# A deformable-convolution layer on one Trainium2 core: scratch copies tripled, one stage of work moved forward by part of an image

## The chip, the cores and the metric

The kernel runs on one core of one Trainium2 chip. The metric is the device time of one execution in microseconds (us); lower is better. All data are float32.

## The reference, cut to what matters

The program is a chain of four residual layers over a batch of 8 images of 384 channels and 32 x 32 pixels. Each layer adds to x the result of a block on the group-normalized x: attention over pixels (layer 0), three deformable depthwise convolutions with a channel gate (layer 1), attention over channels (layer 2), a sum of large depthwise convolutions (layer 3). Only layer 1 matters here:

```python
def deform_block(x, ow, ob, dw, pw, pb, K):
    pad = K // 2
    offsets = conv2d(x, ow, ob, pad)            # 2*K*K offset channels per pixel
    out = deform_depthwise(x, offsets, dw, K, pad)
    return conv2d(out, pw, pb, 0)               # 1x1

def deform_depthwise(x, offsets, w, K, pad):
    # for every tap k: sample x bilinearly at (pixel + tap + offset_k), zero outside,
    # multiply by the channel's weight w[:, k], and add up over the K*K taps
    ...

c3, c5, c7 = jnp.split(x, 3, axis=1)            # 128 channels each
out3 = deform_block(c3, ..., 3)
out5 = deform_block(c5, ..., 5)
out7 = deform_block(c7, ..., 7)
out = jnp.concatenate([out3, out5, out7], axis=1)
return out * se_weight(out, fc1_w, fc2_w)
...
x = x + layer1(group_norm(x))
```

## The kernel before, in words

Layers 0, 2 and 3 stand before and after layer 1 in the program and are not changed. Layer 1 (`layer1`) does bilinear sampling as matrix products. It walks 8 images (`b`), in each the three kernel sizes 3, 5 and 7 (`r` = 0, 1, 2; "kernel of 7" is r = 2), and in each kernel size the output columns in strips (`s`): four strips for 3, four for 5, ten for 7. The taps' rows are taken in groups: one group for 3, two for 5 and two for 7. A task is one (image, kernel size, strip, group); an image has 4 + 8 + 20 = 32 of them.

What a task needs is prepared by two stages that run beside the tasks, each ahead of them:

- `offsets(b, r)`: normalizes the 128 channels, transposes them on TensorE (line 569), writes them as small overlapping patches into a DRAM scratch image (`im`, line 593), and makes the offsets with one matmul per tap (line 621: 9 taps for 3, 25 for 5, 49 taps in two halves for 7). The weights of these matmuls (`cw`, line 549) are loaded `AHEAD` chunks in front. The positions (`pos`) go to DRAM (line 639).
- `hats(b, r)`: turns positions into bilinear weights, called hats. For each kx, and for 7 for each of two parts (rows and columns), one piece: load `d` from `pos` (line 657), take the absolute distance on ScalarE (line 673), take max(0, 1 - distance) on ScalarE (line 685), write the result to the DRAM scratch `hat` (line 703). The loads of `d` run one piece in front.

The tasks then do the sampling:

- `load_columns` (line 745, SyncE's queue) and `load_rows` (line 765, GpSimd's queue) bring the hats of task i + 2 from DRAM (`hx` and `s`), `patches` (line 721, GpSimd's queue) brings the patches `xw`.
- `sample_weights` spreads the column hats over partitions with a selection matrix on TensorE (`columns`, line 786; the matrix is `sel`, whose entries `SEL` lists) and multiplies them into the row hats on VectorE (line 789).
- `sample` multiplies patches with these weights on TensorE (`v`, line 826); ScalarE copies the sums out (`z`, line 834).
- `accumulate` multiplies by the tap's weight and adds on VectorE (`acc`, line 860).
- `end` does the 1 x 1 convolution (line 880, taken out by line 881) and, after the kernel of 7, the channel gate; it reads the results and x again (`or`, `xr`) and writes x back (line 922).

The order of all instructions in layer 1 is written out by hand (`manual_schedule`), so that each engine and each DMA queue runs them in program order. For each slot of a task the loop works out how much of the image is `done`, once by a measure called `room` and once by one called `cost`, and then advances each stage until it has as many steps as `PLAN` asks for. `PLAN` holds points (done, share of the stage's work), one list for offsets (by room) and one for hats (by cost), and is read by straight lines between points. In cost the kernel of 3 ends at 0.1 of an image, that of 5 at 0.381.

By these points the hats of the kernel of 7 of the next image are made from 0.79 of an image to 0.31 of the next one, and the hats of 3 and 5 from 0.31 to 0.79. The offsets run 1.3 images in front of the tasks, so that those of the kernel of 7 of the next image begin as the image begins.

The scratch images and hats have two copies, chosen by `b % 2`. Those of images are zeroed at their borders in layer 0 by `clear`, on GpSimd's queue.

Of the kernel before, what the change touches and what calls it, by code (L numbers as in the profile page):

```python
# [40 lines left out]
class Cells:  # L41
# [69 lines left out]
SEL = [(w, m, j) for w in sorted({c.wx for c in CELLS}) for m in range(1, 32 // w + 1) for j in range(m)]  # L111
SGAP = 32
WCH = 4
AHEAD = 5
# [29 lines left out]
def kernel(ctx: ExitStack, tc: tile.TileContext, t, out):  # L144
# [341 lines left out]
    def layer1(x2):  # L486
        with tc.tile_pool(name="l1w", bufs=1) as wp, tc.tile_pool(name="l1", bufs=2) as sp, tc.tile_pool(
# [24 lines left out]
            for i in range(2):  # L512
                h = wp.tile([P, max(g.pitch for g in CELLS) * H], F32, tag=f"hs{i}", name=f"hs{i}")
                nc.vector.memset(h, 0.0)
                hs.append(h)
# [3 lines left out]
            for i in range(3):  # L519
                s = wp.tile([P, SROW + 2 * SGAP], F32, tag=f"s{i}", name=f"s{i}")  # L520
                nc.vector.memset(s, 0.0)
                weights.append(s)
# [12 lines left out]
            def offsets(b, r):  # L535
# [25 lines left out]
                im = images[r, b % 2]  # L561
# [75 lines left out]
                pos = dpool.tile([n2, N], F32, tag=f"pos{r}", name=f"pos_{b}_{r}", bufs=2)  # L637
# [4 lines left out]
            def hats(b, r):  # L642
# [9 lines left out]
                def load(kx, part):  # L652
                    d = sp.tile([P, N], F32, tag="d", name=f"d_{b}_{r}_{kx}_{part[0]}")
                    at = 0
                    for a in part:
                        w = (g.wy, g.wx)[a]
                        nc.sync.dma_start(
                            d[at : at + ks * w],
                            bass.AP(
                                tensor=pos.tensor, offset=pos.offset + (2 * kx + a) * N, ap=[[0, w], [2 * ks * N, ks], [1, N]]  # L660
                            ),
                        )
                        at += ks * w
                    return d, at

                ahead = load(*todo[0])
                yield
                for j, (kx, part) in enumerate(todo):
                    d, n = ahead
                    if j + 1 < len(todo):  # L670
                        ahead = load(*todo[j + 1])
# [23 lines left out]
                    for a in part:  # L695
                        w = (g.wy, g.wx)[a]
                        for hat, lo in zip(hatsof[r, a, b % 2], (0, g.last and g.last[0])):
                            if not lo <= kx < lo + hat.shape[3]:
                                continue
                            s0 = 0 if hat is hatsof[r, a, b % 2][0] else g.strips - 1  # L700
# [9 lines left out]
            def patches(b, r, s):  # L710
# [5 lines left out]
                im = images[r, b % 2]  # L716
# [14 lines left out]
            def load_columns(i, b, r, s, k0, k1):  # L731
# [5 lines left out]
                tiles = hatsof[r, 1, b % 2]  # L737
# [15 lines left out]
            def load_rows(i, b, r, s, k0, k1):  # L753
# [5 lines left out]
                tiles = hatsof[r, 0, b % 2]  # L759
# [807 lines left out]
```

## Time and profile before

| | us |
|---|---|
| median of three runs | 8086.81 |
| lowest and highest | 8068.79, 8088.71 |
| the profiled execution's own time | 8090.77 |
| its span, first to last instruction | 8088.9 |

| engine in the span | busy us | share |
|---|---|---|
| PE (matmul) | 6941.8 | 86% |
| DVE (VectorE) | 3995.6 | 49% |
| ACT (ScalarE) | 2448.4 | 30% |
| POOL (GpSimd) | 1087.7 | 13% |

The mean granted TensorE clock is 0.896 of full speed. The DMA queues moved 1119 MB; the queue of GpSimd took 26.0% of the 16 engines' span and that of SyncE 19.9%. Layer 1 runs from about 2440 to 6690 us, some 510 us an image once it is under way.

A row of busy time by stretches gives, for each engine, the busy us and the number of instructions. A line in the chain of waits gives start, length and what the chain went through. In a timeline the brackets at the end of a line hold the engine's idle time before it and what ended that. SP and SPq are SyncE and its DMA queue; PEld is the load of a matmul's weights.

### The profile page before, as it was taken

How to read it: one execution, taken by the hardware profiler on the slowest of the kernel's cores; microseconds unless marked ns; L12 is line 12 of the kernel's file. 1: busy time of each engine (PE TensorE's matmuls, PEld its weight loads, DVE VectorE, ACT ScalarE, POOL GpSimd, SP SyncE). 2: the span in 40 equal slices, each digit the busy share in tenths (PEclk: the TensorE clock that was granted, in tenths of full speed). 3: DMA queues.
4: the chain of work that ended last, by engine and by line, in shares of the span. 5: the costliest groups of instructions: out<-in, count | busy, mean ns of one | idle time of the engine just before them, and what ended most of it. 6: DMA issues, size and time to landing. Idle time of an engine off the chain costs nothing.

```text
span 8088.9 us, 99749 instructions
## 1 busy us (share of the span) xinstructions
PE 6941.8 (86%) x38761; PEld 3835.8 (47%) x38761; DVE 3995.6 (49%) x7839; ACT 2448.4 (30%) x4587; POOL 1087.7 (13%) x2052
## 2 busy tenths in 40 slices
PE   8999999999986798798998989989799786888664
PEld 4434444444433355455555545555456464545342
DVE  4433433334332356575766757667577682222322
ACT  2232332332222333433434334343344330111000
POOL 0000000000001022222222222222222220000001
PEclk9999999999987898898988989989898887888787
DMA  1110000000006677878878788787887851000343
GB/s 55 23 48 29 20 10 22 20 7 15 15 22 197 185 208 203 256 220 257 233 206 273 218 258 235 216 274 216 259 237 224 242 155 69 32 32 16 96 117 115
DMA packets 529699, 1119.27 MB, mean 138 GB/s; under 512 B 160208, under 2 KB 386872, under 8 KB 489828
## 3 DMA queue, kind: packets, MB, share of 16 engines
q0 software_dynamic: 150880, 626.06, 26.0%
q1 hardware_dynamic: 370688, 467.37, 19.9%
q10 hardware_dynamic: 7652, 19.38, 0.7%
q8 instruction: 310, 5.08, 0.3%
q14 instruction: 169, 1.38, 0.1%
HBM read 888.01 MB, written 223.77 MB: 137 GB/s over the span
## 4 chain that ended last, share of the span: by engine, by line
PE 69%; DMA 15%; DVE 8%; issue 3%; ACT 2%; SPq 1%; POOL 1%; ACTq 0%; DVEq 0%; POOLq 0%
PE v L826 14%; PE po L621 10%; PE columns L786 7%; PE s L400 6%; PE s L384 6%; PE pa L409 6%; PE pqk L1255 3%; DMA s<-hat 3%; PE pc L1369 2%; DMA hx<-hat 2%; PE pq L368 2%; DVE acc L860 2%; PE po L439 2%; PE pk L368 2%; DMA xw<-im 2%
## 5 line engine op out<-in xcount | busy, mean ns | idle before, releaser
L826 PEld LDWEIGHTS v<-s,xw 120*128 120x128 f32 (+1 forms) x10560 | 1624.0, 204 | 1130.5 <-issue 645.5
L826 PE MATMUL v<-s,xw 120*128 120x126 f32 (+6 forms) x10560 | 1949.7, 327 | 210.8 <-ACT z L834 96.9
L834 ACT ACTIVATE z<-v 128x336 f32<-128x336 f32 (+6 forms) x2360 | 1095.0, 473 | 2383.6 <-PE v L826 2199.6
L860 DVE SCALAR_TENSOR_TENSOR acc<-z,dw,acc 128x128 f32<-128x128 f32 (+6 forms) x4504 | 1677.4, 377 | 125.4 <-ACT z L834 0.5
L789 DVE TENSOR_TENSOR s<-s,columns 120x896 f32<-120x896 f32 (+3 forms) x816 | 936.2, 1147 | 1387.6 <-PE columns L786 1266.1
L386 DVE TENSOR_REDUCE mx<-s 128x1 f32<-128x512 f32 x1024 | 640.4, 683 | 1109.3 <-PE s L384 1108.8
L621 PE MATMUL po<-xp,cw 128*98 128x512 f32 (+2 forms) x2944 | 1088.8, 592 | 16.1 <-ACT off L629 8.9
L786 PE MATMUL columns<-hx,sel 30*120 30x448 f32 (+6 forms) x3776 | 862.9, 599 | 238.5 <-DMA hx<-hat 134.1
L765 POOL DMA_DIRECT2D s<-hat x960 | 509.4, 545 | 2947.2 <-PE v L826 1291.2
L402 ACT ACTIVATE e<-s 128x512 f32<-128x512 f32 x1024 | 537.3, 601 | 1046.9 <-PE s L400 1035.6
L721 POOL DMA_DIRECT2D xw<-im x864 | 466.4, 578 | 1848.4 <-DVE off L635 1787.4
L400 PE MATMUL s<-q,k 49*128 49x512 f32 x2048 | 600.0, 637 | 53.4 <-DMA q<-both 53.4
L384 PE MATMUL s<-k,q 49*128 49x512 f32 x2048 | 599.1, 668 | 5.3 <-ACT e L402 2.1
L409 PE MATMUL pa<-e,va 128*49 128x512 f32 x2048 | 549.3, 611 | 18.2 <-ACT e L402 18.2
L786 PEld LDWEIGHTS columns<-hx,sel 30*120 30x120 f32 (+3 forms) x3776 | 265.4, 193 | 616.7 <-issue 246.9
L384 PEld LDWEIGHTS s<-k,q 49*128 49x128 f32 x2048 | 331.7, 317 | 278.9 <-issue 171.0
L400 PEld LDWEIGHTS s<-q,k 49*128 49x128 f32 x2048 | 253.6, 199 | 317.4 <-issue 202.9
L1369 PE MATMUL pc<-xT,hk 32*32 32x232 f32 (+6 forms) x9984 | 239.9, 428 | 178.7 <-issue 99.6
L621 PEld LDWEIGHTS po<-xp,cw 128*98 128x98 f32 (+2 forms) x2944 | 300.6, 151 | 171.8 <-issue 126.3
L409 PEld LDWEIGHTS pa<-e,va 128*49 128x49 f32 x2048 | 117.4, 124 | 370.1 <-issue 326.3
L1369 PEld LDWEIGHTS pc<-xT,hk 32*32 32x32 f32 x9984 | 169.4, 112 | 248.9 <-issue 160.3
L1255 PE MATMUL pqk<-wqk,xn 128*128 128x384 f32 x768 | 271.9, 519 | 9.5 <-DVE xn L256 8.4
(145 smaller groups left out, 3985.3 us busy)
## 6 DMA issues: line engine op xcount, KB each, us to landing
s<-hat POOLq DMA_DIRECT2D x288, 448.0 KB, 9.6
xw<-im POOLq DMA_DIRECT2D x608, 208.0 KB, 10.0
s<-hat POOLq DMA_DIRECT2D x288, 336.0 KB, 7.0
s<-hat POOLq DMA_DIRECT2D x128, 540.0 KB, 9.5
s<-hat POOLq DMA_DIRECT2D x128, 360.0 KB, 8.5
hat<-hs SPq DMA_DIRECT2D x112, 378.0 KB
s<-hat POOLq DMA_DIRECT2D x128, 324.0 KB, 7.4
x<-x SPq DMA_DIRECT2D x24, 1536.0 KB
```

The costliest lines, as they stand in the source:

```text
L384: mm(ps[j], lhsT=q[rows, n:N:QCH], rhs=k[rows, hs], start=True, stop=True)
L386: nc.vector.tensor_reduce(mx[:, j, n, h : h + 1], ps[j], AX.X, ALU.max)
L400: mm(ps[j], lhsT=k[rows, n * P : (n + 1) * P], rhs=q[rows, hs], start=True, stop=True)
L402: nc.scalar.activation(state["e", n % 2, j][:, hs], ps[j], AF.Exp, scale=HD**-0.5)
L409: mm(pa[rows, halves[h]], lhsT=va[:, n, 2 * g + j, :], rhs=state["e", n % 2, j][:, halves[h]], start=(n == 0), stop=(n == QCH - 1),)
L621: mm(po[i * g.pm : (i + 1) * g.pm, :n], lhsT=cw[:, k, :], rhs=xp[:, y0 : y0 + n // W, x : x + W], start=(ky == 0 and kx == 0), stop=(ky == ...
L786: mm(columns[: g.q, c, :n], lhsT=sel[rows, k, : g.q], rhs=hx[rows, :n], start=True, stop=True)
L789: nc.vector.tensor_tensor(dst, dst, columns[: g.q, : g.parts, :n], ALU.mult)
L826: mm(dst[:, (lo - k0) * nk : (hi + 1 - k0) * nk, :, xl * g.tw : (xl + 1) * g.tw], lhsT=state["xw", b, r, s][: g.q, xl, p0 + j, :], rhs=rhs ...
L834: nc.scalar.activation(z[:, :, yy : yy + n * g.th, :].rearrange("p k (j t) x -> p j k (t x)", j=n), v.rearrange("p j (k f) -> p j k f", k= ...
L860: nc.vector.scalar_tensor_tensor(dst, z[:, (ky - k0) * nk + kx - first, ky - i0 * g.th : ky - i0 * g.th + H, bx : bx + x1_ + 1 - x0], dw[: ...
L1369: mm(ps[32 * j : 32 * j + 32, i, lo * B : hi * B], lhsT=hk[32 * i : 32 * i + 32, j, (RL - d) * PITCH : (RL - d) * PITCH + W], rhs=xT[32 * ...
```

## The change

It gives images, hats and positions three copies in place of two (`AT = 3`). It moves the points of `PLAN`: offsets run 1.55 images in front in place of 1.3; the hats of 3 and 5 of the next image are made from 0.31 to 0.62 of an image, those of 7 from 0.62 to 1.05. The weights by which `room` spreads offsets over the kernels of 3 and 5 go from 1.5 and 2 to 2 and 3. The loads of `d` run two pieces in front, with three buffers. `SEL` lists only the entries in use (seven in place of nine), the offset weights run 4 chunks in front in place of 5, and the memsets of `hs` and of the three weight buffers `s` are issued on GpSimd in place of VectorE.

```diff
-SEL = [(w, m, j) for w in sorted({c.wx for c in CELLS}) for m in range(1, 32 // w + 1) for j in range(m)]
+SEL = sorted(
+    {
+        (c.wx, m, j)
+        for c in CELLS
+        for k0, k1 in c.groups
+        for m in {min(c.deep, k1 + 1 - k) for k in range(k0, k1 + 1, c.deep)}
+        for j in range(m)
+    }
+)
 SGAP = 32
 WCH = 4
-AHEAD = 5
+AHEAD = 4
+AT = 3
 
 STEP = 0.3
 PLAN = (
-    ((0, 0.095), (0.035, 0.3), (0.22, 1.02), (0.78, 2.02), (1.3, 2.6), (B - 1.3, B)),
-    ((0, 0.15), (0.035, 0.15), (0.07, 0.388), (0.225, 0.388))
-    + tuple((b + x, b + y) for b in range(B) for x, y in ((0.31, 1.0), (0.79, 1.388)) if b + y <= B),
+    ((0, 0.095), (0.035, 0.3), (0.22, 1.02), (0.78, 2.02), (1.45, 3.0), (B - 1.55, B)),
+    ((0, 0.15), (0.035, 0.15), (0.07, 0.388), (0.225, 0.388), (0.31, 1.0), (0.79, 1.388), (1.28, 2.0))
+    + tuple((b + x, b + y) for b in range(1, B) for x, y in ((0.31, 1.0), (0.62, 1.388), (1.05, 2.0)) if b + y <= B),
 )
...
-        for i in range(2):
+        for i in range(AT):
             images[r, i] = dpool.tile([g.cols, g.wy, g.ny, P], F32, tag=f"im{r}{i}", name=f"im{r}{i}")
...
                 h = wp.tile([P, max(g.pitch for g in CELLS) * H], F32, tag=f"hs{i}", name=f"hs{i}")
-                nc.vector.memset(h, 0.0)
+                nc.gpsimd.memset(h, 0.0)
...
                 s = wp.tile([P, SROW + 2 * SGAP], F32, tag=f"s{i}", name=f"s{i}")
-                nc.vector.memset(s, 0.0)
+                nc.gpsimd.memset(s, 0.0)
...
-                im = images[r, b % 2]
+                im = images[r, b % AT]
...
-                pos = dpool.tile([n2, N], F32, tag=f"pos{r}", name=f"pos_{b}_{r}", bufs=2)
+                pos = dpool.tile([n2, N], F32, tag=f"pos{r}", name=f"pos_{b}_{r}", bufs=AT)
...
-                    d = sp.tile([P, N], F32, tag="d", name=f"d_{b}_{r}_{kx}_{part[0]}")
+                    d = sp.tile([P, N], F32, tag="d", name=f"d_{b}_{r}_{kx}_{part[0]}", bufs=3)
...
-                ahead = load(*todo[0])
+                ahead = [load(*todo[j]) for j in range(2)]
                 yield
                 for j, (kx, part) in enumerate(todo):
-                    d, n = ahead
-                    if j + 1 < len(todo):
-                        ahead = load(*todo[j + 1])
+                    d, n = ahead.pop(0)
+                    if j + 2 < len(todo):
+                        ahead.append(load(*todo[j + 2]))
...
-                steps = (1.5, 2, 7 if k0 else 4)[r] * (min((s + 1) * g.nc, g.nx) - s * g.nc) / g.nc
+                steps = (2, 3, 7 if k0 else 4)[r] * (min((s + 1) * g.nc, g.nx) - s * g.nc) / g.nc
```

The other places where `b % 2` chose a copy of hats or images read `b % AT` in the same way.

More of the change, by code (lines that the diff above doesn't have):

```diff
@@ L696, in hats @@
                         w = (g.wy, g.wx)[a]
-                        for hat, lo in zip(hatsof[r, a, b % 2], (0, g.last and g.last[0])):
+                        for hat, lo in zip(hatsof[r, a, b % AT], (0, g.last and g.last[0])):
                             if not lo <= kx < lo + hat.shape[3]:
                                 continue
-                            s0 = 0 if hat is hatsof[r, a, b % 2][0] else g.strips - 1
+                            s0 = 0 if hat is hatsof[r, a, b % AT][0] else g.strips - 1
                             ns = hat.shape[0]
@@ L715, in patches @@
                 state["xw", b, r, s] = xw
-                im = images[r, b % 2]
+                im = images[r, b % AT]
                 for x in range(s * g.nc, min((s + 1) * g.nc, g.nx)):
@@ L736, in load_columns @@
                 n = tap // g.parts
-                tiles = hatsof[r, 1, b % 2]
+                tiles = hatsof[r, 1, b % AT]
                 hat = tiles[0][s] if nk == g.ks else tiles[1][0]
@@ L758, in load_rows @@
                 wt = weights[i % 3]
-                tiles = hatsof[r, 0, b % 2]
+                tiles = hatsof[r, 0, b % AT]
                 hat = tiles[0][s] if nk == g.ks else tiles[1][0]
```

## The prediction

> **What bounds the kernel now.** I read the slices of the span first: layer 1 is the part from 2440 to 6690 us, with the DMA at 6 to 8 tenths and the PE at 8 to 9. Layers 0, 2 and 3 keep their code, so what follows is layer 1 alone. The ends of the three kernel sizes of an image are seen in the ACT rows of line 881 (4259, 4333, 4450 and 4767 us for image 3), so I asked for the busy time in exactly those stretches, and in the same stretches of the last image.
>
> ```profile
> 4261.00:4335.00 74.00, 49.24 (x240) 32.11 (x239) 34.46 (x54) 27.59 (x56) 16.07 (x31) 0.82 0.99 316
> 4335.00:4451.00 116.00, 107.81 (x461) 65.14 (x462) 84.08 (x129) 54.91 (x122) 28.29 (x54) 0.93 0.82 242
> 4451.00:4769.00 318.00, 297.12 (x1536) 175.31 (x1536) 214.57 (x507) 117.06 (x218) 80.60 (x153) 0.95 0.76 219
> 6251.00:6322.00 71.00, 39.90 (x218) 26.94 (x216) 34.30 (x53) 24.77 (x51) 16.16 (x31) 0.78 0.91 286
> 6322.00:6428.00 106.00, 92.17 (x427) 59.59 (x425) 84.45 (x130) 50.68 (x116) 26.49 (x50) 0.92 0.77 239
> 6428.00:6683.00 255.00, 211.39 (x1101) 152.31 (x1100) 198.33 (x490) 78.54 (x159) 68.98 (x130) 0.82 0.60 159
> ```
>
> Columns: stretch, length, busy PE, PEld, DVE, ACT, POOL, then granted clock, DMA share, GB/s. Row 1 is image 3's kernel of 3: DMA full (0.99), PE idle for 25 of 74 us. Row 2, its kernel of 5: idle for 8. Row 3, its kernel of 7: DMA 0.76, PE idle for 21 of 318. Rows 4 to 6 are the last image, which makes no hats in its kernel of 7 and no offsets at all. Summing the PE's busy time times its clock over 10 us slices gives its work at full clock: 42, 101 and 284 us (427 of the 508). So 54 us of an image are idle PE and about 27 are lost to a low clock. The DMA is busy for 73 + 95 + 241 = 409 us: what is wrong is its spread, not its sum.
>
> What runs beside the kernel of 3 is in the chain of waits for 4100 to 4460 us:
>
> ```profile
> 4125.38 11.96 DMA hx<-hat
> 4137.72 16.61 DMA hx<-hat
> ...
> 4280.53 20.63 DMA im<-xT
> ...
> 4306.05 14.73 DMA x<-xr
> 4321.18 7.00 DMA or<-od
> ```
>
> The image write of the next image's kernel of 7 (im), the end of the image before (xr, or) and the hats of 7 meet there. The two hx lines lie in the second half of the kernel of 7, just after the image write of the next kernel of 3. What such a stall costs the clock is in the PE's timeline:
>
> ```profile
> 4154.47 2.06 PE L786 MATMUL columns<-hx,sel 30*120 30x448 f32 x4 [8.50 <-DMA hx<-hat]
> 4158.99 1.85 PE L786 MATMUL columns<-hx,sel 30*120 30x448 f32 x4
> 4162.97 1.85 PE L786 MATMUL columns<-hx,sel 30*120 30x448 f32 x4
> 4179.12 1.01 PE L786 MATMUL columns<-hx,sel 10*120 10x448 f32 x4
> ```
>
> After 8.5 idle us four column matmuls take 1.85 us where they otherwise take 1.01, and they are back at 1.01 only 25 us later. [...] The rows show about 22 us at half speed, so about 11 lost: I price such a stall at 20 us. [...]
>
> **The change, part by part.** *Where the hats of 7 are made.* They are 14 pieces an image (7 kx, two parts); per image 14 x 378 + 7 x 315 + 4 x 42 KB are written and 7 x (336 + 280) KB of d read: 12.0 MB. What is a megabyte worth? The kernel of 7 has 241 us of DMA in image 3 and 153 in the last image; the 88 between them are, added up from the DMA issues, about 25 MB (hats of 3 and 5: 7, half the hats of 7: 6, offset weights: 5, two image writes: 4, the rest: 3), 3.5 us a MB. So the hats of 7 are 42 us of DMA. The ACT rows of line 673 put seven pieces into the kernel of 7 (4640 to 4764 us), three into the next kernel of 3 (4784 to 4828), four into its kernel of 5 (to 4888). With the new points (0.62, 1.388) and (1.05, 2.0), 12 pieces fall into the kernel of 7 in front and two into the first tasks of 3. So about 9 us of DMA leave the kernel of 3 and 12 that of 5, and 21 enter that of 7. All of a piece moves: loads of d, ACT's two steps, the writes, always on SP's queue.
>
> *Offsets earlier, third copies.* By the new points the image write of 7 (four copies of 0.5 MB, 7 us by that rate) comes at 0.8 of the image in front, beside the kernel of 7. There the two-copy buffer would still be read; the third copy is what lets it go. The room of (2, 3) for (1.5, 2) moves some 14 of 98 offset matmuls from the kernel of 7 into those of 3 and 5: 14 x 0.43 us = 6 us of PE. The extra zeroing (three images, one pair of hats) lies in layer 0 on POOL, whose zeroing steps there wait only for DVE and where the DMA is 1 tenth busy: nothing, and at most the 0.5 us issue of some 30 more DMAs if the cover were gone.
>
> *New stage times.* Kernel of 3: DMA 73 - 9 - 7 = 57 us, PE work 42 + 3. Before, the stage took 1.01 (74 for 73.1) to 1.09 (70 for 64.2) of its DMA time; at 1.05 it is 60 us, against a mean of 72 over four images (74, 70, 73, 69): -12. Late next there are the tail's loads. Kernel of 5: PE work 104, DMA 83; of some 12 us lost before (mean stage 112) most stays as wait for weights; I take -6. Kernel of 7: PE work -6. Its DMA becomes 241 + 21 + 7 = 269 in 318 us, 0.85, spread evenly. Its first half (4451 to 4620, hats of 3 and 5, share 0.78) loses 1 us of idle, its second (hats of 7 and two image writes) 20. If loss goes with hat pieces, it doubles: +20 idle and +13 of clock; if with image writes, a third one adds 10. The chain shows the hx waits right behind an image write, so I take +8, less 6: +2, ends -6 and +27.
>
> Sum: images 2 to 6 gain 18 each (-90); six kernels of 7 (images 1 to 6) pay 2 (+12); the last image, where no image write leaves, gains 12 in its 3 (70 to 58) and 12 in its 5 (106 to 94, work 85): -24. Image 1 still makes its 7's hats late (point 1.28): 0. Together -102, ends -226 (rival C below) and +48 (the +27 in all six).
>
> *Memsets to POOL.* At the start of layer 1 DVE is the chain:
>
> ```profile
> 2406.75 1.12 DVE L514 MEMSET hs<- 128x1280 f32 x1 [0.22 <-issue]
> 2408.09 1.12 DVE L514 MEMSET hs<- 128x1280 f32 x1 [0.21 <-issue]
> 2410.07 3.71 DVE L521 MEMSET s<- 128x4384 f32 x1 [0.86 <-issue]
> 2424.51 0.68 DVE L256 TENSOR_SCALAR xs<-xs,mr 128x1024 f32<-128x1024 f32 x1
> ```
>
> With the two later memsets of s, 16.4 us go from before line 256. Does POOL become the bound? The trace has no POOL memset of this size; DVE's rows sum to 13.4 us. [...] Queued behind are the xw loads (2424 instead of 2440 otherwise, needed only at 2460) and the first s loads (2461.7, then 2445). Above 3.05 times, 41 us, POOL would be late; [...] hidden, -16, ends -17 and +12.
>
> *Loads of d two ahead.* ACT's wait for d (total, times, longest) is the row
>
> ```profile
> ACT d L673 <- DMA d<-pos: 151.0, 26, 16.7
> ```
>
> In images 3 and on it is some 9 us an image, already in the idle time counted above; the long ones are in images 0 and 1, and the PE feels part of them: -10, ends -40 and 0. A load issues before the hat writes of the piece in front on SP, but waits for the relu two pieces back, which is done: no new wait. ACT and DVE work is unchanged. *Four chunks of offset weights ahead, smaller sel:* 4 chunks are 14 taps, about 30 us in the steady kernel of 7; only image 0, with 24 taps a task, is close: +3, ends 0 and +10.
>
> Total: -102 - 16 - 10 + 3 = -125. The profiled execution took 8090.8 us (span 8088.9), so 7966; the median of the runs, 8086.8, is 4 lower: 7962.
>
> **Rivals.** *A, slower: hx behind the hats on SP.* SP is in order; in the second half of 7 each of 13 tasks now writes a hat piece, and the next task's hx loads queue behind. Volume can't do it (269 us of DMA x 1.09 = 293, under 318), order can: with n more stalls of 20 us an image, six kernels of 7 pay 6 x (20n - 6), against 137 gained elsewhere; from n = 1.4 on it is slower. With three: +187, 8274. For it: the hx lines at 4125 and 4137. Against: the first half makes hats of 5 at a full PE. Chance 0.12.
>
> *B, the kernel of 3 stays as it is,* since tail transfers and loads keep it late one by one, and 5 and 7 just even out. Then only start and d remain: -23, 8064. For it: x<-xr and or<-od in the chain. Against: they come at a full DMA. Chance 0.12.
>
> *C, everything clears:* kernel of 3 to 50 us, of 5 to 103, of 7 only -6: -5 x 31 - 6 x 6 - 35 - 26 = -252, 7835. For it: PE work is then all there is. Against: the DMA's 409 us would fill 0.87 of the 471 that are left. Chance 0.2.
>
> Main case 0.56. About 0.3% (24 us) is what a measurement of this kernel tells from no change. Faster by more: main, C and the luckier half of B, 0.81; within: 0.08; slower: 0.11. The range leaves out A and the far ends: 7820 to 8085.
>
> **What would show it.** Right: kernel-of-3 stretches of 55 to 60 us with DMA under 0.97; no im write of 7 inside them; 84- and 70-row abs steps all between 0.62 and 1.05 of an image; the kernel of 7 at a DMA share near 0.85 and 310 to 325 us; normalize 16 us earlier at the start; almost no ACT wait for d. Wrong: several hx waits of over 5 us in each second half of 7, or a kernel of 3 still over 68 us.

## The result: slower by 1.3%, and the profile after

The changed kernel takes 8192.0 us (median of four runs, 8183.0 to 8205.4) against 8087.8 for the kernel before in the same comparison: a ratio of 1.0134, 95% interval 1.0111 to 1.0156. Forecast were 7962 us. In the tables and sums below one profiled execution stands for a kernel; such a one lies up to 36 us from the median of its kernel's runs. The profiled execution has a span of 8181.1 us (8088.9 before) and a mean granted clock of 0.891 (0.896).

The six stretches that the prediction opened with, now in the changed kernel: image 3's kernels of 3, 5 and 7, then the last image's. Columns: stretch, length, busy PE, PEld, DVE, ACT, POOL, granted clock, DMA share, GB/s.

```profile
4314.00:4384.00 70.00, 50.60 (x239) 31.84 (x237) 34.36 (x54) 18.06 (x40) 15.86 (x30) 0.82 0.85 262
4384.00:4501.00 117.00, 110.05 (x474) 65.31 (x475) 84.10 (x129) 49.05 (x115) 28.21 (x54) 0.96 0.72 211
4501.00:4843.00 342.00, 304.14 (x1526) 180.45 (x1525) 214.96 (x508) 134.10 (x242) 81.89 (x154) 0.90 0.80 229
6354.00:6421.00 67.00, 40.06 (x218) 27.01 (x216) 34.38 (x54) 17.76 (x40) 16.23 (x31) 0.80 0.85 271
6421.00:6524.00 103.00, 90.52 (x423) 59.84 (x421) 83.91 (x129) 42.55 (x103) 28.31 (x54) 0.92 0.68 205
6524.00:6781.00 257.00, 219.94 (x1105) 158.96 (x1104) 199.49 (x491) 78.69 (x159) 67.20 (x127) 0.80 0.59 158
```

The DMA moved as the change says: its share falls from 0.99 to 0.85 in the kernel of 3 and from 0.82 to 0.72 in that of 5, and rises from 0.76 to 0.80 in that of 7. The time did not follow. The kernels of 3 and 5 of image 3 take 70 and 117 us (74 and 116 before), and its kernel of 7 takes 342 (318 before), with the PE idle for 38 us of it (21 before) and at a lower clock when it runs (0.90 for 0.95).

Between the same two events (the end, on the PE, of the first half of the 1 x 1 convolution of each kernel size), the 99 us by which layer 1 ends later add up as follows: the start of layer 1, up to the end of its first kernel of 3, -16, the rest of image 0 +6, image 1 +47, images 2 to 5 +18 each, image 6 -4, image 7 -4. (With the end of the second half as the mark, 11 us go over from image 1 to image 0: +36 and +17.) In images 2 to 5 the kernel of 7 alone is +23 (321 to 344), that of 3 is -6, that of 5 +1.

**Where the kernel of 7 stands.** All gaps of the PE in it, added up by what ended them, as a mean over images 2 to 5 (us an image):

| gap ended by | before | after |
|---|---|---|
| DMA hx (column loads) | 9.4 | 16.5 |
| DVE s (products of hats) | 6.8 | 10.2 |
| ACT z (evictions) | 0 | 7.7 |
| DVE xs (normalize) before the transposes | 0 | 3.1 |
| the rest | 3.1 | 2.9 |
| sum | 19.3 | 40.4 |

The 7.1 us more of hx and the 7.7 us of z both stand behind an image write: in each of images 1 to 5 there is one z gap of 6.9 to 9.0 us at the write for a kernel of 3 and one hx gap of 11.5 to 14.8 us at the write for a kernel of 7. Both writes belong to the image after next. Not only the write for 7 has moved: by the longer lead and the new room those for 3 and 5, which lay at 0.6 and 0.75 of the kernel of 7, now lie at 0.23 and 0.4 of it, and that for 7 at 0.65.

Here is the write of image 5's kernel of 7, which the change has put beside image 3's kernel of 7; SP's queue first, then the PE. Columns of a timeline: start, length, engine and line, operation, tiles; in brackets the idle time before it and what ended that.

```profile
4721.15 8.06 SPq L602 DMA_DIRECT2D im<-xT  x7
4729.26 2.33 SPq L712 DMA_DIRECT2D hat<-hs  x2
4731.69 9.44 SPq L602 DMA_DIRECT2D im<-xT  x4
4747.63 2.44 SPq L754 DMA_DIRECT2D hx<-hat  x4
```

```profile
4753.28 1.97 PE L795 MATMUL columns<-hx,sel 30*120 30x448 f32 x4 [11.74 <-DMA hx<-hat]
4759.01 1.01 PE L795 MATMUL columns<-hx,sel 30*120 30x448 f32 x4
```

The last four image DMAs alone hold SP for 9.4 us, 7.8 of them in the issue of the first one; the median issue in layer 1 takes 0.6 us (0.43 for the `place` load behind them). Another 3.7 us pass before its next chunk of weights, and the hx loads of the next task come out 15.9 us after the last four began. The PE stands for 11.7. After it the column matmuls are at their full speed by the second row, 6 us later.

The write of image 5's kernel of 3, earlier in the same stage, hurts by another engine. First SP, then ScalarE, then the PE's row at the end of it:

```profile
4574.80 12.18 SPq L602 DMA_DIRECT2D im<-xT  x8
4587.61 3.03 SPq L754 DMA_DIRECT2D hx<-hat  x4
```

```profile
4578.43 0.45 ACT L843 ACTIVATE z<-v 128x336 f32<-128x336 f32 x1 [2.77 <-DVE acc L869]
4589.48 0.59 ACT L584 ACTIVATE xT<-pt 64x512 f32<-64x512 f32 x1 [10.60 <-DMA im<-xT]
4591.01 1.10 ACT L843 ACTIVATE z<-v 128x336 f32<-128x336 f32 x3
```

ScalarE wants to evict the fourth transposed piece (xT) of the image; xT has three buffers, and the first is free only when its DMAs have landed. For 10.6 us it stands there, and the z evictions that the PE needs are queued behind. At 4591.49 us the PE comes out of a gap of 7.9 us.

SP's 12.2 us are mostly a wait too. Seven of the eight DMAs are issued by 4579.7 us, the eighth at 4586.7. What SP waited for between 4574 and 4592 us (total, times, longest):

```profile
SPq L602 <- DMA hat<-hs: 7.2, 2, 6.9
```

That is a hat write which SP had issued at 4574.1, eight DMAs in front. This holds throughout: in layer 1 none of SP's 2,304 DMAs (2,310 before the change) was issued until the one eight places in front of it had landed. So a few large writes that land late keep the small loads behind them from being issued, here for 6.9 us.

**Where the kernel of 3 stands.** Its hx gap (10.4 us an image before) is gone, and another has come in its place, before the 1 x 1 convolution (`pp<-acc,pw`): 10.0 us an image (2.7 before). DVE's and PE's rows:

```profile
4377.38 1.28 DVE L930 SCALAR_TENSOR_TENSOR xr<-or,gate,xr 128x1024 f32<-128x1024 f32 x1 [11.63 <-DMA or<-od]
4380.05 2.04 PE L889 MATMUL pp<-acc,pw 128*128 128x512 f32 x2 [10.83 <-DVE acc L869]
```

The chain of waits has the same place as two DMAs one after the other, where before it had im, x and or at a full DMA:

```profile
4357.81 9.37 DMA x<-xr
4367.62 9.66 DMA or<-od
```

DVE reaches the tail of the image in front, whose `or` load has not landed, and stands for 11.6 us with its last accumulations (acc) queued behind. Taking the hats of 7 and the image write out of this stage did not bring that load forward: the kernel of 3 lost 14 us of DMA time and won 6 us.

**The start of layer 1** went as forecast. POOL's zeroing of s and DVE's first normalize:

```profile
2407.11 11.13 POOL L530 MEMSET s<- 128x4384 f32 x3
```

```profile
2414.86 3.94 DVE L265 TENSOR_SCALAR xs<-xs,mr 128x1024 f32<-128x1024 f32 x1
```

And ScalarE's row for d has halved, from 151.0 us to this (total, times, longest):

```profile
ACT d L682 <- DMA d<-pos: 70.6, 13, 14.4
```

### The profile page after: what moved, and what is told of

Read it like the earlier page. It is cut to its first block, busy times and chain, and to the rows that moved or that the text cites. A ratio compares the mean times of both kernels' runs of the same rounds, so it can differ in the third digit from the quotient of the medians.

```text
span 8181.1 us, 99772 instructions
## 1 busy us (share of the span) xinstructions
PE 7011.0 (86%) x38761; PEld 3870.8 (47%) x38761; DVE 3986.2 (49%) x7834; ACT 2453.8 (30%) x4587; POOL 1119.1 (14%) x2089
## 4 chain that ended last, share of the span: by engine, by line
PE 67%; DMA 16%; DVE 10%; issue 3%; ACT 2%; SPq 1%; POOL 1%; ACTq 0%; DVEq 0%; POOLq 0%
PE v L835 13%; PE po L630 8%; PE columns L795 7%; PE s L409 6%; PE s L393 6%; PE pa L418 6%; DVE acc L869 3%; PE pqk L1264 3%; DMA s<-hat 3%; DMA hx<-hat 3%; PE pc L1378 2%; DVE s L798 2%; PE pq L377 2%; PE po L448 2%; PE pk L377 2%
## 5 line engine op out<-in xcount | busy, mean ns | idle before, releaser
L835 PEld LDWEIGHTS v<-s,xw 120*128 120x128 f32 (+1 forms) x10560 | 1644.1, 206 | 1149.6 <-issue 659.0
L835 PE MATMUL v<-s,xw 120*128 120x126 f32 (+6 forms) x10560 | 1977.0, 330 | 187.1 <-ACT z L843 87.9
L630 PE MATMUL po<-xp,cw 128*98 128x512 f32 (+2 forms) x2944 | 1113.7, 599 | 18.9 <-DMA cw<-in_ow_dram 10.3
L1378 PE MATMUL pc<-xT,hk 32*32 32x248 f32 (+6 forms) x9984 | 244.1, 437 | 176.3 <-issue 100.8
```

The source lines that it names most:

```text
L630: mm(po[i * g.pm : (i + 1) * g.pm, :n], lhsT=cw[:, k, :], rhs=xp[:, y0 : y0 + n // W, x : x + W], start=(ky == 0 and kx == 0), stop=(ky == ...
L835: mm(dst[:, (lo - k0) * nk : (hi + 1 - k0) * nk, :, xl * g.tw : (xl + 1) * g.tw], lhsT=state["xw", b, r, s][: g.q, xl, p0 + j, :], rhs=rhs ...
L1378: mm(ps[32 * j : 32 * j + 32, i, lo * B : hi * B], lhsT=hk[32 * i : 32 * i + 32, j, (RL - d) * PITCH : (RL - d) * PITCH + W], rhs=xT[32 * ...
```

## The experiments

The theory at the start: image writes, three in a kernel of 7 instead of two, send a burst down SP's queue in front of hx, and that is the loss. The rivals: the hats' new place; the volume of the DMA; the longer lead of the offsets. "The small edits" below are the zeroing on POOL, d two loads ahead, four chunks ahead and the smaller sel, with the old points, the old room and two copies. All numbers of stages are means over images 2 to 5 of one profiled execution (us); a ratio is that of the medians of the timed runs to the kernel before on the same chip. A difference of two ratios, turned into us below, is uncertain by 15 to 35 us. Where writes are left out (e8, e9, e19 to e21), it is from image 3 on.

| kernel | ratio (95%) | 3 | 5 | 7 | PE idle in 7 | image 1 |
|---|---|---|---|---|---|---|
| before | 1 | 72 | 114 | 321 | 20 | 522 |
| changed | 1.0134 (1.0111 to 1.0156) | 66 | 116 | 344 | 40 | 569 |
| e1 small edits | 0.9978 (0.9965 to 0.9990) | 71 | 118 | 324 | 21 | 511 |
| e2 hats at old points | 1.0097 (1.0076 to 1.0118) | 66 | 115 | 342 | 34 | 559 |
| e3 image write of 7 kept in 3 | 1.0287 (1.0267 to 1.0307) | 87 | 114 | 348 | 35 | 557 |
| e4 image writes on ACT | 1.0122 (1.0099 to 1.0145) | 65 | 116 | 350 | 41 | 557 |
| e8 no image write of 7 | 1.0040 (1.0023 to 1.0057) | 66 | 113 | 335 | 32 | 544 |
| e9 the same on e1 | 0.9946 (0.9926 to 0.9967) | 70 | 113 | 322 | 20 | 521 |
| e10 image writes dealt out | 1.0075 (1.0052 to 1.0098) | 67 | 115 | 345 | 37 | 573 |
| e11 hats moved alone | 1.0039 (1.0022 to 1.0056) | 72 | 108 | 337 | 24 | 545 |
| e12 fourth xT buffer | 1.0173 (1.0135 to 1.0210) | 67 | 115 | 355 | 46 | 557 |
| e13 e11, first abs later | 1.0028 (1.0016 to 1.0040) | 71 | 113 | 333 | 25 | 536 |
| e14 old room | 1.0169 (1.0137 to 1.0201) | 69 | 110 | 355 | 36 | 571 |
| e15 fourth xT buffer on e1 | 1.0049 (1.0033 to 1.0066) | 75 | 114 | 332 | 27 | 527 |
| e16 e1, idle loads in 7 | 0.9971 (0.9959 to 0.9982) | 71 | 116 | 323 | 20 | 510 |
| e17 e1, new room | 1.0041 (1.0024 to 1.0058) | 79 | 116 | 333 | 31 | 531 |
| e18 e1, idle loads in 5 | 0.9988 (0.9977 to 0.9998) | 73 | 115 | 322 | 17 | 517 |
| e19 no writes of 7's hats | 1.0084 (1.0060 to 1.0107) | 65 | 116 | 339 | 37 | 571 |
| e20 no image writes | 0.9970 (0.9957 to 0.9982) | 65 | 115 | 322 | 21 | 538 |
| e21 the same on e1 | 0.9910 (0.9887 to 0.9933) | 69 | 115 | 315 | 16 | 506 |

**The halves of the change.** The small edits alone:

> The kernel before plus only the small edits: memsets of hs and s on POOL, loads of d two pieces ahead with three buffers, the shorter sel, offset weights four chunks ahead. Plan, room weights and two copies stay as before. All theories of the changed kernel's loss (it took 92 us more in its profile, of which about +23 an image in the kernels of 7 of images 2 to 5 and +47 in image 1) put it into the moved stages, so here 8060 to 8080 us, 10 to 25 faster than before: about 13 at the start of layer 1 (the normalize of line 265 stood 3.3 us behind the POOL memset in the changed kernel) and a few from the waits for d. If the d loads or the shorter look-ahead of weights were to blame, it is slower than before by 50 or more.

As expected: 0.9978, 18 us under the kernel before, and nearly all of it the start. By the ratios that is 126 us under the changed kernel, (1.0134 - 0.9978) x 8087.8, and no other version that computes everything is measurably faster: of the whole change, this part is the one to keep.

The hats' old points, all else changed:

```diff
-    ... ((0.31, 1.0), (0.62, 1.388), (1.05, 2.0)) ...
+    ... ((0.31, 1.0), (0.79, 1.388)) ...
```

> The changed kernel with the hat points of before, so the hats of 7 are made from 0.79 to 0.31 again; offsets stay 1.55 images ahead with the new room weights and three copies. Hat-piece theory (seven more hat pieces beside the kernel of 7 load SP's queue and the DMA): the kernels of 7 fall back from 344 to about 322 us, those of 3 rise from 65 to 71, in all about 8110. Image-write theory (it is the image write of the next kernel of 7, now at 0.8 of an image, that keeps hx from being issued): the kernels of 7 stay at 338 or more, those of 3 rise, 8190 to 8220. Lead theory (offsets of images 0 and 1 are made 0.25 image earlier, which lengthens image 1 by 27 us of PE and gives nothing back later): image 1 stays at about 570 us in both.

1.0097: putting the hats back returns 30 us of 126 (uncertain by 25). The offsets' new lead and room cost some 96 without the hats (1.0097 less 0.9978). The other way round, the hats' move with the offsets' old lead and room:

```diff
-    ... (1.45, 3.0), (B - 1.55, B)),
+    ... (1.3, 2.6), (B - 1.3, B)),
-    ... ((0.31, 1.0), (0.62, 1.388), (1.05, 2.0)) ...
+    ... ((0.31, 1.0), (0.74, 1.388), (1.06, 2.0)) ...
-                steps = (2, 3, 7 if k0 else 4)[r] * ...
+                steps = (1.5, 2, 7 if k0 else 4)[r] * ...
```

> The changed kernel with the offsets' old lead (1.3) and old room (1.5, 2), so that the image write of 7 is back in the kernel of 3 at its old place, and with the hats of 7 still made in the kernel of 7 of the image in front (0.74 to 1.06, as the old lead has the positions only then). It is the hats' move alone, at an unchanged pace of the offsets. If the image write and the lead cost the time, it comes near the small edits alone, 8081 us, less a few us of each kernel of 3 and 5: 8040 to 8085. If the hats' move costs it: 8150 and more, with the kernels of 7 at 335 and more.

1.0039, so 49 us over the small edits: the time lies between the two expectations, and the kernels of 7 are where the second put them (337). Against the kernel before, the kernel of 5 gives the forecast 6 us (114 to 108), the kernel of 3 nothing, and each kernel of 7 loses 16. The two halves alone make 49 + 96 = 145, together 126, so they share part of what they cost.

**Keeping the image write of 7 where it was.** This also takes the old room (1.5, 2) and makes the offsets of 7 by the middle of the image, so more than one thing moves.

```diff
-(0.78, 2.02), (1.45, 3.0), (B - 1.55, B)),
+(0.78, 2.02)) + tuple((b + x, b + y) for b in range(1, B) for x, y in ((0, 1.308), (0.5, 2.0)) if b + y <= B),
```

> The changed kernel with another offset plan: from image 1 on the offsets of 7 start with the image, as before (image write beside the kernel of 3), and are done at half of the room, in time for the hats of 7 at 0.62; room weights 1.5 and 2 as before, which puts as many offset matmuls (33) into the kernels of 3 and 5 as the change does. Hats as in the change. Image-write theory: kernels of 7 fall from 344 to about 325, those of 3 rise from 65 to about 69; with a lead of 1.31 image 1 loses less: 8070 to 8100. Hat-piece theory: kernels of 7 stay at 338 to 345, those of 3 rise: 8170 to 8200. Lead theory: image 1 falls from 570 to about 540 us either way.

Much slower, 1.0287, against the simple form of the theory. The write lies in the kernel of 3 again, at 0.1 of it instead of 0.25 to 0.4, and that kernel now takes 87 us:

```profile
4334.95 7.18 SPq L603 DMA_DIRECT2D im<-xT  x7
4350.60 10.99 SPq L755 DMA_DIRECT2D hx<-hat  x6
```

```profile
4365.81 2.26 PE L796 MATMUL columns<-hx,sel 32*128 32x480 f32 x6 [21.39 <-DMA hx<-hat]
```

What SP waited for in the same stretch (4334 to 4367 us; total, times, longest):

```profile
SPq L755 <- DMA im<-xT: 6.4, 5, 1.6
```

hx gaps of 21.6 us in each kernel of 3 (10.4 before). The DMA share of that stage was lower than before (0.78 for 0.97), so a full DMA is not the reason: five of the six hx loads could each be issued only when one more DMA of the image write had landed. And the kernel of 7 didn't get better for losing this write; its z gaps rose to 12.2 us.

**Other places for the same writes.** On ScalarE's queue instead of SP's:

```diff
                         for w, copies, use in places:
...
-                            nc.sync.dma_start(
+                            nc.scalar.dma_start(
```

> The changed kernel with the image writes (line 602) issued on ACT's DMA queue in place of SP's; bytes and plan the same. If the loss is the order on SP (hx behind image and hat writes), the hx waits of 12 to 15 us in the kernels of 7 go and these fall from 344 to 320 to 330: 8060 to 8110. If it is the DMA's load, hx waits stay and it takes 8180 to 8200. If ACT is held up while it issues[...], the waits turn into waits of v for z and it is as slow or slower.

1.0122, within the interval of the changed kernel: the third expectation, with the transposes (pt) in place of v. hx gaps in the kernel of 7 fall from 16.5 to 2.7 us an image, as they should, and the transposes now stand for 22.5 us behind ScalarE:

```profile
4606.09 0.86 ACTq L602 DMA_DIRECT2D im<-xT  x2
4607.00 0.59 ACT L584 ACTIVATE xT<-pt 64x512 f32<-64x512 f32 x1 [10.17 <-DMA hat<-hs]
```

```profile
4607.65 1.06 PE L578 MATMUL pt<-cst,xs 128*64 128x128 f32 x4 [6.76 <-ACT xT L584]
```

The gap has changed its name; the sum is the same, 40 us of gaps an image on SP's queue and 41 on ScalarE's. ScalarE stands there because its own image DMA, too, has to wait until a hat write of SP has landed (the 10.17 us of the row). The record of the changed kernel shows that the two queues count together: their 2,874 DMAs have eight semaphores between them, with 359 or 360 on each. The DMA's own time did not fall by the other queue, 276 us in the stage for 272.

Dealt out, a whole step of the planner after each image DMA:

```diff
+                            yield 1
...
-                sum(g.ks**2 * max(1, g.pn // HALF) + STEP * ...
+                33 + sum(g.ks**2 * max(1, g.pn // HALF) + STEP * ...
```

> The changed kernel with the DMAs of an image write dealt out: after each of the 10 to 12 the planner counts one whole step, so that they spread over about two tasks and let the tap and patch loads of the tasks through between them, in place of one burst. Same work, same bytes. If the burst in front of the next loads is what costs, each kernel of 7 loses two or three stalls less of about 20 us: idle PE from 38 to about 20 us in it, 8192 - 6 x 30 = 8010 us. If the volume or the earlier offsets cost it, nothing: within 20 us of 8192, or worse, as each image's offsets then take longer.

1.0075, 48 us better in the timed runs, but a quarter of what was expected; the profiled execution (span 8188.9), the slowest of its four runs, shows a kernel of 7 of 345 us and no gain, so where the 48 us lie is not shown.

A fourth buffer for xT:

```diff
-                    xT = sp.tile([P, 4, P], F32, tag="xT", ..., bufs=3)
+                    xT = sp.tile([P, 4, P], F32, tag="xT", ..., bufs=4)
-AHEAD = 4
+AHEAD = 2
```

> The changed kernel with a fourth buffer for the transposed image pieces (xT), so that ScalarE no longer waits for the first piece's image DMAs before it evicts the fourth; to make room, two chunks of offset weights ahead in place of four. In the changed kernel ScalarE stands 10.6 us at that wait with the next z behind it (PE gap of 7.9 us at 4591 us), once in each kernel of 7. If that is half of the loss there: kernels of 7 from 341 to about 325 us, 8192 - 6 x 16 = 8095 us. If the taps' loads behind the same burst are late anyway, the gap only changes its name (hx for z) and the time stays within 20 us of 8192.

> The kernel before with the small edits alone and the fourth xT buffer (two chunks of offset weights ahead). In its kernels of 7 no gap is put down to z; the gaps at an image write are hx's (3.9 and 6.4 us). So if the fourth buffer matters only by ScalarE's order: 8081 within 10 us. If it lets the burst out earlier and so ends it earlier: 8081 - 6 x 5 = 8050.

The small edits lose 57 us by it (1.0049 for 0.9978); against the changed kernel the loss is not clear of noise (1.0173 for 1.0134). The traces say what happened: the z gaps of the changed kernel's kernel of 7 are gone (0 for 7.7 us an image), so the wait for an xT buffer was their cause. In their place the hx gaps rose from 16.5 to 20.2 us, and 9.4 us of gaps wait for offset weights (11.8 in the small edits, where there were none), the price of the two chunks. What the buffer is worth by itself in time stays open.

**The hats' own cost.** In e11 the gap of the kernel of 7 that the kernel before has not is z again, and this time ScalarE waits for the first d of the hats of 7, read from positions that were only just written:

```profile
4622.78 1.15 ACT L682 ACTIVATE d<-d,cst 84x1024 f32<-84x1024 f32 x1 [7.30 <-DMA d<-pos]
```

```profile
4624.45 2.00 PE L835 MATMUL v<-s,xw 120*128 120x126 f32 x8 [5.24 <-ACT z L843]
4626.39 1.85 PE L795 MATMUL columns<-hx,sel 30*120 30x448 f32 x4
```

So three more steps between a unit's first loads and its first abs (the count of steps and the first points of the hats' plan follow):

```diff
                 ahead = [load(*todo[j]) for j in range(2)]
-                yield
+                for _ in range(4):
+                    yield
```

> The hats' move alone, as before (old lead, old room), but with three more steps between the first loads of d of a unit and its first abs. In the run without it ScalarE waits 7.3 us for the first d of the 7's hats, which is loaded from positions just written; z queues behind it, the PE stands for 5.2 us and then runs at half clock for 20 us. If this one wait is what the hats' move costs, the kernels of 7 fall from 337 to about 325 us and the time by 6 x 12 = 72, to about 0.995 to 0.997 of the kernel before. If the hats' volume in the kernel of 7 costs it, no change: 1.004.

1.0028 for 1.0039: no change that the intervals hold apart. The d wait is gone and z is still late by 5.4 us an image. Later in the same stage SP's queue held a hat write behind an image write, and ScalarE stood for the hat buffer:

```profile
4662.53 10.54 SPq L713 DMA_DIRECT2D hat<-hs  x2
```

```profile
4676.61 1.68 ACT L695 ACTIVATE hs<-d 70x32 f32<-70x32 f32 x3 [7.67 <-DMA hat<-hs]
```

```profile
4678.68 1.49 PE L836 MATMUL v<-s,xw 120*128 120x168 f32 x4 [7.73 <-ACT z L844]
```

Two DMAs took SP 10.5 us, 9.9 of them the second one's issue. Hats and image writes meet on SP's queue, and in both rows ScalarE, which waits for a buffer, carries the delay on to the PE.

**Is it the volume?** Over these runs the kernel of 7's length could be read as following its DMA time (242 us of DMA: 321; 262: 337; 272: 344; 280: 355). To try that alone, 30 loads of 0.2 MB that nobody reads, in each kernel of 7 of the small edits:

```diff
+                if i < len(tasks) and 0 < tasks[i][0] < 7 and tasks[i][1] == 2:
+                    for k in range(2 if tasks[i][3] == 0 else 1):
+                        fill = dpool.tile(...)
+                        nc.sync.dma_start(fill, t["ow2"][:, (2 * i + k) % 7, :WCH])
```

> The kernel before with the small edits alone, and 30 more loads of 0.2 MB (offset weights, DRAM to a scratch place in DRAM, read by nobody) in each kernel of 7 of images 1 to 6, dealt out evenly, two or one to a task, on SP's queue behind the task's loads. They add some 21 us of DMA time to its 244 (0.2 MB x 30 x 3.5 us) and no work, no wait and no change of order elsewhere. Prediction's reading (a kernel of 7 takes DMA up to a share of 0.85 for nothing): 321 to 325 us, time within 10 us of 8081. Rival (over the runs so far its length follows its DMA time, 242 to 321, 262 to 337, 272 to 344, 280 to 355: about 0.9 us for each): 342 us and 8081 + 6 x 18 = 8190.

It does not follow. Image 3's kernel of 7 with the idle loads, then without:

```profile
4403.00:4728.00 325.00, 301.37 (x1531) 176.85 (x1530) 214.34 (x506) 117.32 (x218) 80.59 (x152) 0.92 0.80 230
```

```profile
4416.00:4738.00 322.00, 302.22 (x1531) 177.67 (x1530) 214.65 (x506) 117.01 (x218) 80.59 (x152) 0.93 0.76 216
```

This is the share (0.80) and the rate (230 GB/s for 229) of the changed kernel's stage of 342 us, at 323 us in the mean over four images and a ratio of 0.9971. The loads brought 15 us of DMA time, not the 21 expected, and the change brought 28 (244 to 272): evenly spread, 15 us of volume cost nothing. In the kernel of 5:

> The same with the idle loads in the kernels of 5 of images 1 to 6: 12 in each, some 8 us of DMA on top of 98 at a share of 0.83. If the kernel of 5 follows its DMA time as the kernel of 7 seems to: 115 to 122 us and 8081 + 6 x 7 = 8123. If it is bound by its PE work (100 us and what it loses): within 10 us of 8081.

115 us for 118 there, and 0.9988, within 8 us of the small edits: no cost either, though only 3 us of DMA time were added. Taking volume away from the changed kernel instead, by leaving out the writes of the 7's hats:

```diff
-                            for w0 in (0, w) if a == 0 and g.rows > w else (0,):
+                            for w0 in () if r == 2 and b > 2 else (0, w) if a == 0 and g.rows > w else (0,):
```

> The changed kernel without the writes of the 7's hats from image 3 on (left out; their loads of d, abs and relu steps, and the order of all else stay). It takes some 8 MB (28 us of DMA by 3.5 us a MB) out of five kernels of 7. If that kernel's length follows its DMA time: 344 to about 320 us and 8192 - 5 x 24 = 8070 us. If the order (ScalarE's and SP's waits behind image writes) is what costs: 338 us, 8192 - 5 x 6 = 8160.

The kernel of 7 falls by 5 us (344 to 339) for 21 us of DMA time, and the time is 40 us lower than the changed kernel's by the ratios (uncertain by 26). That is near the order's expectation and far from the volume's.

**The image writes priced.** The image write of 7 left out, in the changed kernel and in the small edits:

```diff
-                    for j in range(g.th):
+                    for j in range(g.th if r < 2 or b < 3 else 0):
```

> The changed kernel without the DMAs that write the padded image of the kernel of 7, from image 3 on (what they would have written is left out; everything else, the transposes too, is issued as before). It prices one such write where the change puts it, at 0.8 of the image in front. If the image write is what the kernels of 7 lose by (gap of 12 us and then slow PE), five kernels of 7 (images 2 to 6) should go from about 341 to about 320 us (285 to 265 for image 6), the time to about 8192 - 5 x 21 = 8085 us. If they lose by the volume of the hats beside them, the write's own 7 us of DMA go and little else: 8170 us.

> The kernel before with the small edits alone, and without the writes of the padded image of the kernel of 7 from image 3 on (left out, all else issued). There the write falls into the kernel of 3. It prices the same write at its old place. If the kernel of 3 hides it (it waits for the DMA anyway, and the changed kernel freed 20 us of DMA there for 6 us of time), five kernels of 3 go from 71 to about 66 us: 8081 - 25 = 8056. If the write costs the same wherever it lies, 8081 - 5 x 21 = 7976.

1.0134 to 1.0040 is 76 us, 15 for each of the five writes; from 0.9978 to 0.9946 is 26 us, 5 for each (both uncertain by 4 to 5). So the same write costs 15 us beside the kernel of 7 and 5 beside the kernel of 3. The five lie in images 1 to 5, not 2 to 6 as expected, and image 6 keeps its length (285 and 286 us). A kernel of 7 without the write still takes 335 us against 324: the rest is not this write's. All three left out (`b < 3` alone in that line):

> The changed kernel without the writes of all three padded images from image 3 on (left out; transposes, evictions and all else issued as before). Summed over the gaps of its kernels of 7, the changed kernel loses 7.7 us an image to z and 16.5 to hx, both behind image writes, where the kernel before loses 0 and 9.4. If the image writes are the whole difference, the kernel of 7 falls from 344 to about 315 us (idle 40 to 16) and equals that of the next run; if the rest (hats, lead, order of the steps) holds a share of its own, it stays over 325.

> The same writes left out of the kernel before with the small edits alone. There two of the three lie in the kernel of 7 and one in that of 3. If image writes cost by the piece: 324 to about 308 us in the kernel of 7, and 71 to 68 in that of 3; the time about 8081 - 5 x 18 = 7990 us. If only some placements cost: the kernel of 7 to 316 or more.

The kernels of 7 are now 322 and 315 us: of the 20 us between the two plans 13 lie in the image writes, and the z gap is gone. In time the plans stay 49 us apart (0.9970 less 0.9910), of 126 with the writes; in the profiled executions 32 us are image 1's (538 and 506).

**The room.** Old room with everything else changed (e14, the diff), and the new room on the small edits, with the third copies and a lead of 1.285 (e17):

```diff
-                steps = (2, 3, 7 if k0 else 4)[r] * ...
+                steps = (1.5, 2, 7 if k0 else 4)[r] * ...
```

> The changed kernel with the old room (1.5, 2) for the offsets and all else of the change, the longer lead too: some 14 offset matmuls an image go back from the kernels of 3 and 5 to that of 7. If the kernel of 5 is now bound by its PE work, it falls by their 5 us (116 to 110) and the kernel of 3 by 3, while the kernel of 7, which loses 38 us to gaps, takes them in its clock and gaps for less than 6: 8192 - 7 x 4 = 8165. If the new room is right, the same or 10 us more.

> The kernel before with the small edits, the third copies and the new room (2, 3), the hats at their old points and the offsets' lead at 1.285 for 1.3: some 14 offset matmuls an image go from the kernel of 7 to those of 3 and 5. With the long lead the new room was worth 35 us. If it is worth as much here: 8045 us, faster than both kernels. If the kernel of 3 and 5, which wait for the DMA here, only get longer by that work: the same as the small edits alone, 8081.

Neither gain came. In e14 the kernel of 5 does as said, 110 us for 116, so its offset matmuls are paid in full there. But the kernel of 7 gets 11 us longer for 7 us of work; the time, 28 us longer (1.0169), is not clear of noise. On the small edits the new room costs 51 us (1.0041): in the profiled execution, the slowest of its nine, the kernel of 3 goes to 79 us with `pp<-acc,pw` at 17.8 us an image, that of 7 to 333. The image writes lie there nearly where the small edits have them (at about 0.57 and 0.75 of the kernel of 7 and 0.3 to 0.4 of that of 3), so their place doesn't explain it; why the new room costs on one plan and not on the other stays open.

## Why the prediction was wrong, point by point

- **DMA by stage: right.** 57, 83 and 269 us forecast; 56, 82 and 272 measured.
- **Kernel of 7, "+2": the step that failed.** Measured +23: 21 us of idle PE and 8 of clock, less 6 of work. The work was right, and so was, as far as tried, the reasoning on volume (e16: a share of 0.80 costs nothing when it is evenly spread). The mis-sized term is "I take +8" for the loss, 29 in truth. The prediction had the row that said so, hx waits right behind an image write, priced a third write at 10 and then counted eight in all. It also moved the write for 7 alone: that the same lead brings those for 3 and 5 to other places in the stage is in no step. And it had only SP's queue in view: that ScalarE would wait for xT's buffers and hold z behind it is in no step either, and it is a third of the new idle time. Its sign of being wrong, several hx waits of over 5 us in each second half, came as one of 11.5 to 14.8.
- **The price of a stall, 20 us,** held for its own place alone. By the record of the granted clock the full clock came back 23.5 us after the end of the prediction's gap (27.3 us at 0.5 in all), 13 of them without any gap of the PE, and 17.5 to 17.7 us after the gaps at the same place in the next three images. After the four hx gaps at the write for 7 (images 2 to 5 of the changed kernel) it took 5.0 to 11.0 us. Over all gaps of more than 1.5 us in images 2 to 6 of both kernels that time ranges from 3.0 to 23.5 us, and the runs don't show what sets it.
- **Image 1, "0": the second step that failed,** +47. A lead longer by a quarter of an image has to be worked off once, and image 1 did it: 456 us of PE work at full clock for 429. Of these 27 us, 24 went into its kernels of 3 and 5, which became 13 us longer; the other 34 of the 47 are its kernel of 7 (321 to 355), with 3 us more of work and 20 of idle PE. Without any image writes that takes 327. In turn 37 us of work left image 6's kernel of 7 (248 to 210), but shortened it by only 3 (288 to 285): its gaps grew from 19 to 36 us, put down to VectorE's products (18.3) and to the patches (13.5). There is no image write in it, and without any it takes 285 too.
- **Kernel of 3, "-12": half,** -6. The step scaled the stage with its DMA time, 57 x 1.05. The DMA fell as said, and the tail's `or` load, with DVE waiting for it, took the place of hx. The prediction named the tail's loads as next and put no time on them; rival B did.
- **Kernel of 5, "-6": right for the hats** (e11: -6), and eaten by the new room (+6 between e14 and the changed kernel). The room's work was put in at 3 us (101 to 104) and then hidden.
- **Last image, "-24": -4.** The kernel of 3 gave 4 of 12 and that of 5 gave 2 of 12: the DMA left there, 57 us and 70, was not what they wait for.
- **Zeroing on POOL, "-16": right,** 16.6 at the first v matmul (9.5 earlier, though layer 0 ended 7 later). That POOL would be in time was the author's estimate; the trace before shows no zeroing of this size on it. It takes 11.13 us for the three, 3.71 each, as DVE did (3.71).
- **d two ahead, "-10", and four chunks, "+3":** e1 is 18 us better, of which the start is 16: about -2 for both together, which is within noise. The wait for d did halve (70.6 us in e1 too); the PE had hardly felt it.
- **Rival A** had the mechanism's kind (SP's order, not volume; in layer 1 of the kernel before, SP issued its 2,310 DMAs one after another) and a chance of 0.12. It blamed the hats' writes. The hats' move by itself costs 49 us (e11), though leaving their writes out gives back only 40 (e19); leaving the image writes out takes 77 of the 126 us between the two plans away (e20, e21). These shares overlap and don't add up to the whole. Of rival C, in which everything clears, nothing came.

What stays open: why one placement of an image write costs 5 us and another 15. The traces show what waits behind it on SP and on ScalarE in each place; no run predicts the price from the task it falls in. Open, too, is what makes up the 49 us that remain between the plans without image writes.

## What to carry to other kernels

Ask of a transfer that is moved not only how busy the DMA is where it goes, but which small, urgent loads come next on its queue, which engine waits for its buffer with whose work behind it, and how many transfers may be under way at once (here never more than eight of SP's). A stage at a DMA share of 0.76 took 15 us more of evenly spread loads for nothing (e16: 323 us for 324, and a ratio of 0.9971 for 0.9978); one burst of 2 MB in the changed kernel's stage at 0.80 cost 15 us of time (e8). Where a plan is moved earlier, count the pass in which the lead is built up.

## What the runs showed of the hardware that was not expected

- In this program the DMAs of SP and ScalarE share eight semaphores (2,874 DMAs, 359 or 360 on each), and none of SP's 2,304 in layer 1 was issued before the one eight places in front had landed. That wait is 6.9 of the 12.2 us for eight DMAs of an image write, and 6.4 of the 11.0 us over which e3 issues its six hx loads.
- One issue can itself hold SP: 7.8 us of the 9.4 for four DMAs of an image write, 9.9 of the 10.5 for two of a hat behind such a write (e13), where the median in layer 1 is 0.5 to 0.6. No run shows what decides it.
- A zeroing of 128x4384 takes POOL 3.71 us, the same as VectorE. Beside it VectorE's normalize took 3.94 us where it had taken 0.68, and it ended at 2418.8, just after POOL's 2418.2. No run shows what held it.
